# Output tiles between the last pairs' value products, two reads moved: a gated cross-attention block on one Trainium2 core

## The chip, the core and the metric

The kernel runs on one core of one Trainium2 chip. The time is device microseconds of one launch. Before the change three runs took 1480.28, 1481.79 and 1483.81 us; their median, 1481.79 us, is the time before. The profile is of one further execution, of 1480.91 us.

## The reference

32 sequences of 64 tokens attend to a context of the same size, with 32 heads of 128 channels, and a linear layer with low-rank adapters follows. Cut to what is computed:

```
x  = x + tanh(g_xattn) * attn(layernorm(x), ctx, mask, bias)
       q, k, v = layernorm(x) @ Wq, ctx @ Wk, ctx @ Wv         # 512 -> 32 heads x 128
       score   = q k^T / sqrt(128) + bias, masked
       attn    = (softmax(score) @ v) @ Wo                      # 4096 -> 512
x  = x + tanh(g_ffn) * (layernorm(x) @ weight^T + bias + adapter(layernorm(x)))
```

All of it is in fp32.

## The kernel before

The 2048 tokens are done in two phases (`p` = 0, 1) of 1024 tokens, each 8 tiles of 128 tokens. A phase first makes keys and values of all heads (`stage_a`), which go to DRAM, and then runs `attention`, whose inner function `run` goes over 16 pairs of heads, `n` = 0 to 15. After phase 1 the linear layer (`ffn_chunk`) runs over four chunks of 512 tokens.

Every large product is split in a high and a low part: `mm3` (L94 to L101) makes of each term three matmuls, high x high, high x low and low x high. A tile of output of one pair has two terms and so six matmuls of 128x128 by 128x512 into one bank of PSUM; the order inside a tile is (ah,bh), (ah,bl), (al,bh) for the first term, then the same for the second, and `last` puts chosen ones at the end. For pair `n` the parts of the attention are:

- `q_unit(n)`: queries of the pair, 42 matmuls.
- `score(n, ...)` with `scores` (L855): small products of queries and keys, then on VectorE the addition of the bias and a maximum (L863, L865), on GpSimd the subtraction of the maximum (L866), on ScalarE the exponential (L875, through `exped`, one step later).
- `normed` (L879): per head a sum, a reciprocal and a product on VectorE (L885 to L887), then the multiplication of the 128x512 block on GpSimd (L888). `turn` (L899) transposes in blocks of 32 on VectorE and 8 small copies (L896) bring the blocks to their places in `pt` (or `pz`). For the last two pairs all of this is one generator, `last_turned`: at its step 0 and 2 it does `normed` for the two heads of pair 14, at 4 and 5 it transposes these, at 6 and 8 it does `normed` for pair 15.
- `pv(n)`: small products of the turned probabilities with the values (L1010) into four banks; of each bank ScalarE makes the high part (L1014, `ch` or `cx`) and VectorE the low part (L1015, `cl` or `cx`), and after each comes a `beat()`. It then asks for the values of pair `n+1` (L804).
- `prep_o(n)`: the output weights `wo` of a pair are split, high on ScalarE, low on GpSimd (L91, for pair 13 L1034 and L1038), and when both halves are done the next pair's raw weights are fetched (L259), into the same buffer.
- `oproj(n)` and `oproj2(n, ...)`: output tiles `pa`. `oproj2` accumulates two pairs `n` and `n+1` in one bank, and VectorE adds the bank to `acc` (L1074).

The program's order is written out by hand and each engine executes its own instructions in that order. Work that accompanies the matmuls is written as generators in the list `streams`; `beat()` advances every one of them by a step, after each unit or tile. `drain(g)` runs a generator to its end at that place. So the place of a `beat()` decides where, in the queues of VectorE, ScalarE, GpSimd and SP, a step's instructions stand. All DMAs go through SP's queue; one that waits holds up those behind it.

[...] A new tile takes the bank that was given back first, by the program's order; this is how the banks of the built program follow one another, for instance 6, 7, 1, 2 for the scores of pairs 14 and 15 and 4, 3, 5, 0 for the products of pair 13.

At the end of a phase `run` does: the scores of 14 and 15, a beat, the drain of `ob[13]` (which splits `wo` of pair 13), `pv(13)`, then `last_unit` (which adds generators of the next phase, in phase 1 `ffn_weights`), then the tiles of pairs 12 and 13, `pv(14)`, `pv(15)`, and the tiles of pairs 14 and 15. Generators are set aside in `held` while `pv(14)` and `pv(15)` run.

In the linear layer the normalized tokens of phase 1 are turned by `ffn_turn(t)` and stored in DRAM (`xtd`, L1279), and `ffn_load(c, ...)` reads a chunk of them back in four steps of four DMAs each (L1262), one step per beat. `ffn_split` makes the high part on ScalarE and the low part on VectorE (`fa`, L90 and L91), `ffn_lora` does the eight matmuls of the adapters (`pt`, L1286 and L1287), `ffn_out` does a tile (`pf`, 12 matmuls and 2 of L1314, the sum on VectorE at L1316, the store at L1317) and then a beat.

Of the kernel before, what the change touches and what calls it, by code (L numbers as in the profile page):

```python
# [14 lines left out]
ALU = mybir.AluOpType  # L15
AX = mybir.AxisListType

P = 128
# [25 lines left out]
def flamingo_block(ctx: ExitStack, tc: tile.TileContext, x, xT, ctxT, bias, mask, gx, gf,  # L44
# [19 lines left out]
    def beat():  # L64
        for g in list(streams):
            if next(g, True):
                streams.remove(g)

    def drain(g):
        if g is not None and g in streams:  # L70
            streams.remove(g)
            for _ in g:
                pass
# [12 lines left out]
    def psum(name, shape=(P, 512)):  # L86
        return psp.tile(list(shape), F32, tag="ps", name=name)
# [6 lines left out]
    def mm3(ps, terms, start=True, stop=True, last=()):  # L94
        todo = []
        for (ah, al), (bh, bl) in terms:
            todo += [(ah, bh), (ah, bl), (al, bh)]
        todo = [x for k, x in enumerate(todo) if k not in last] + [todo[k] for k in last]
        for i, (a, b) in enumerate(todo):
            nc.tensor.matmul(ps, a, b, start=start and i == 0, stop=stop and i == len(todo) - 1,  # L100
                             skip_group_check=True)  # L101
# [693 lines left out]
    def attention(p, res, rest, qt, freed):  # L795
# [251 lines left out]
        def o_terms(n, t):  # L1047
            h, lo = ctx_of(n)
            w = b["o", n]
            sl = slice(t * P, (t + 1) * P)  # L1050
            return [((h[:, i, sl], lo[:, i, sl]),
                     (w[:, 0, i * 512:(i + 1) * 512], w[:, 1, i * 512:(i + 1) * 512])) for i in range(2)]

        def oproj(n, ts=range(NT)):
            drain(ob.get(n))
            for t in ts:
                ps = psum(f"pa{p}_{n}_{t}")
                mm3(ps, o_terms(n, t))
                nc.vector.tensor_tensor(acc[t], ps, acc[t], ALU.add)  # L1059
                beat()  # L1060


        def oproj2(n, ts, lead, beside=None):
            drain(ob[n])
            ts = list(ts)
            for group in [ts[:lead]] + [[t] for t in ts[lead:]]:
                ps = [psum(f"pa{p}_{n}_{t}") for t in group]
                for k, t in enumerate(group):
                    mm3(ps[k], o_terms(n, t), stop=False)
                    beat()  # L1070
                drain(ob[n + 1])
                for k, t in enumerate(group):
                    mm3(ps[k], o_terms(n + 1, t), start=False)
                    nc.vector.tensor_tensor(acc[t], ps[k], acc[t], ALU.add)  # L1074
                    if n == NPR - 2 and p < NPH - 1:
                        nc.sync.dma_start(out=x1d[t * P:(t + 1) * P, :], in_=acc[t])
                    beat()
                    if beside:
                        beside(t)

        ob, qT = {}, {}

        def start_o(n, wait=0):
            ob[n] = behind(wait, prep_o(n)) if wait else prep_o(n)
            streams.append(ob[n])


        def run(xq, prefetch, before_last, last_unit, values_read, beside=None):
            qb = {}


            def start_q(n, eng=nc.gpsimd, wait=0):
                g = p * NPR + n
                qb[n] = prep("q", g, eng, wait, then=(lambda: fetch("q", g + 1, "r0")) if n + 1 < NPR else None)
                streams.append(qb[n])

            def q_unit(n):
                g = p * NPR + n
                drain(qb.get(n))
                if n == 0:  # L1100
                    start_q(1, nc.vector, 2)
                elif n == NPR - 1:
                    before_last()
                elif n % 2 == 0 or n == 3:
                    start_q(n + 1)
                qT[n] = kqp.tile([P, 2, TP], F32, tag="kq", name=f"qT{g}")
                if n == 1:
                    start_o(0, 2)
                end = unit(wt[("q", g)], xq, None, k_dst(qT[n]), f"q{g}", tuple(carry))
                carry.clear()  # L1110
                end()
                if n % 2 and 3 < n < NPR - 1:
                    start_q(n + 1)

            def score(*ns):
                for n in ns:
                    drain(b.get(("m", n)))
                for n in ns:
                    for i in (0, 1) if n else (1, 0):
                        scores(n, i, qT[n], b["k", n])  # L1120
                for n in ns:
                    if 0 < n < NPR - 2:
                        load_k(n + 2)
                n = ns[0]
                if n == 0:
                    b["s", n] = first_softmax()
                elif n == NPR - 2:
                    b["s", n] = b["s", n + 1] = last_turned()
                else:
                    b["s", n] = both(normed(n, 1), turned(n))  # L1130
                streams.append(b["s", n])
                if 1 < n < NPR - 2:
                    b["n", n + 1] = normed(n + 1, 5)
                    streams.append(b["n", n + 1])

            q_unit(0)
            enter_late()
            b["m", 1] = bias_mask(1)
            score(0)
            streams.append(b["m", 1])  # L1140
            streams.append(load_acc())
            q_unit(1)
            start_q(2)
            pv(0)
            score(1)
            oproj(0)
            q_unit(2)
            start_o(1)
            pv(1)
            q_unit(3)  # L1150
            score(2, 3)
            for a in range(4, NPR, 2):
                oproj(a - 3)
                q_unit(a)
                start_o(a - 2)
                pv(a - 2)
                q_unit(a + 1)
                if a < NPR - 2:
                    oproj(a - 2)
                start_o(a - 1)  # L1160
                if a < NPR - 2:
                    pv(a - 1)
                else:
                    drain(b["s", a - 1])
                    next(ob[a - 1])
                    held = list(streams)
                    streams.clear()
                score(a, a + 1)
                if a == NPR - 8:
                    streams.append(paced(prefetch(), 4))  # L1170

            n = NPR - 4
            load_v(n + 3)
            beat()
            streams.append(ob[n + 1])
            drain(ob[n + 1])
            pv(n + 1)
            streams.extend(g for g in held if g is not ob[n + 1])
            last_unit()
            start_o(n + 2, 3)  # L1180
            oproj2(n, range(4), 4)
            start_o(n + 3, 3)
            oproj2(n, range(4, NT), 1)
            drain(ob[n + 3])
            drain(b["s", n + 3])
            held = list(streams)
            streams.clear()
            pv(n + 2)
            pv(n + 3)
            streams.extend(held)  # L1190
            values_read(acc)
            oproj2(n + 2, range(NT), 2, beside)

        return enter, run

# [39 lines left out]
    def ffn_weights(tags):  # L1235
        wf = [big(tags[i], [P, KT, 512], F32R, f"wf{i}") for i in range(2)]
        ffn_w.update(wf=wf, tags=tags)
        streams.append(ffn_load(0, tags[6]))
        ar, br, a2 = ffn_w["ar"], ffn_w["br"], ffn_w["a2"]

        b2 = ffn_w["b2"] = [wbp.tile([P, 512], F32R, tag="wb", name=f"b2{i}") for i in range(2)]
        for _ in range(8):
            yield
        nc.scalar.copy(b2[0], br)
        nc.scalar.copy(b2[1][64:P, :], br[64:P, :])
        nc.gpsimd.tensor_tensor(b2[1][0:64, :], br[0:64, :], b2[0][0:64, :].bitcast(F32), ALU.subtract)
        yield
        nc.scalar.copy(a2[:, :, 0:NL * R], ar)
        nc.gpsimd.tensor_tensor(a2[:, :, 64:64 + NL * R], ar, a2[:, :, 0:NL * R].bitcast(F32), ALU.subtract)
        yield  # L1250
        for kt in range(KT):
            split(ffn_w["raw"][:, kt, :], wf[0][:, kt, :], wf[1][:, kt, :], nc.gpsimd)
            yield
        streams.append(paced(x1_load(1), 2))
# [75 lines left out]
    for p in range(NPH):  # L1330
# [34 lines left out]
        else:  # L1365
# [29 lines left out]
            def load(c, tag):  # L1395
# [6 lines left out]
                          3: [(ffn_turn, 4)]})  # L1402
            ffn_chunk(1, {0: [(ffn_turn, 5)],
                          1: [(ffn_turn, 6)],
                          2: [(ffn_turn, 7), (ffn_split, 2, 0, 1)],
                          3: [(load, 3, "f0"), (ffn_split, 2, 2, 3)]})
            ffn_chunk(2, {2: [(ffn_split, 3, 0, 1)],
                          3: [(ffn_split, 3, 2, 3)]})
            ffn_chunk(3)
# [45 lines left out]
```

## Time and profile before

| what | value |
|---|---|
| median of three runs | 1481.79 us |
| profiled execution, its own time | 1480.91 us |
| its span | 1479.1 us |
| TensorE (PE) busy | 1467.4 us, 99% |
| GpSimd (POOL) busy | 1051.8 us, 71% |
| VectorE (DVE) busy | 938.2 us, 63% |
| ScalarE (ACT) busy | 713.8 us, 48% |
| granted clock of TensorE | 1.0 |
| one 128x128 by 128x512 matmul of a `pa` tile, start to start | 0.227 us |
| `pv` of one pair, unstalled | 2.02 to 2.04 us |

The page of a profile gives busy times, what moved by DMA, the chain of work that ended last, and groups of instructions with the idle time before them. The timeline lists the instructions of one engine in order of time, merged where one follows another: start, duration, engine, line, operation, what is written from what, the count, and in brackets the idle time before it and what ended that. "issue" there means that the engine waited for nothing that the profile shows. The view of the waits lists who waited for whom: total, number of times, longest.

### The profile page before, as it was taken

To read this page: it belongs to the slowest core of one execution; us is meant where nothing else is said; L and a number is where in the kernel's file an instruction comes from. 1 tells how busy PE (TensorE), PEld (TensorE's weight loads), DVE (VectorE), ACT (ScalarE), POOL (GpSimd) and SP (SyncE) were. 2 spreads that over 40 slices of the span, in tenths; PEclk is the share of its full clock that TensorE was granted. 3 is DMA by queue.
4 is the path that set the end of the run, shared out by engine and by line. 5 is a ranking of instruction groups with operands and counts; after the bars stand their busy time and mean duration, and the time that the engine had idled before them with its cause. 6 is when DMAs were issued, how large, how long until landed. Compare 5 with 4: busy or idle time off the path is not lost.

```text
span 1479.1 us, 31285 instructions
## 1 busy us (share of the span) xinstructions
PE 1467.4 (99%) x12008; PEld 1221.3 (83%) x12008; DVE 938.2 (63%) x1589; ACT 713.8 (48%) x1582; POOL 1051.8 (71%) x1160
## 2 busy tenths in 40 slices
PE   9999999999999999999999999999999999999998
PEld 7888888888888888888888888888888888888887
DVE  5675464367776677676379756436767667767774
ACT  5444233346645664576334423334655566557611
POOL 4899378968766676778889947896876767677420
PEclk9999999999999999999999999999999999999999
DMA  5754544475443455352385664447544345535454
GB/s 204 285 203 163 183 174 165 142 276 175 159 156 122 151 193 194 112 190 93 141 288 208 235 218 178 172 142 256 188 155 166 117 155 183 204 117 178 116 145 111
DMA packets 148343, 259.38 MB, mean 175 GB/s; under 512 B 44417, under 2 KB 78209, under 8 KB 144098
## 3 DMA queue, kind: packets, MB, share of 16 engines
q1 hardware_dynamic: 147906, 256.87, 50.3%
q8 instruction: 94, 1.54, 0.4%
q10 hardware_dynamic: 288, 0.52, 0.1%
q14 instruction: 55, 0.45, 0.1%
HBM read 179.74 MB, written 77.61 MB: 174 GB/s over the span
## 4 chain that ended last, share of the span: by engine, by line
PE 94%; DMA 2%; SPq 1%; POOL 1%; ACT 1%; issue 1%; DVE 1%; POOLq 0%; ACTq 0%; DVEq 0%
PE pa L100 22%; PE pvv L100 6%; PE pxv L100 6%; PE pzv L100 6%; PE pxq L100 6%; PE pvq L100 6%; PE pzk L100 6%; PE pvk L100 6%; PE pxk L100 6%; PE pzq L100 6%; PE po L1010 4%; PE ps L861 4%; PE pyv L100 3%; PE pyq L100 3%; PE pyk L100 3%; PE pf L100 2%
## 5 line engine op out<-in xcount | busy, mean ns | idle before, releaser
L100 PE MATMUL pa<-wo,ch 128*128 128x512 f32 x896 | 278.4, 392 | 0.7 <-ACT ch L1014 0.4
L896 ACT COPY pt<-tp 32x256 f32<-32x256 f32 x452 | 182.4, 404 | 69.7 <-DVE tp L899 60.1
L100 PEld LDWEIGHTS pa<-wo,ch 128*128 128x128 f32 x896 | 166.8, 188 | 36.2 <-ACT ch L1014 0.7
L100 PE MATMUL pa<-wo,cl 128*128 128x512 f32 x448 | 174.9, 390 | 0.2 <-DVE cl L1015 0.2
L1059 DVE TENSOR_TENSOR acc<-pa,acc 128x512 f32<-128x512 f32 x192 | 129.4, 681 | 53.4 <-PE pa L100 53.4
L815 POOL TENSOR_TENSOR sm<-sm,madd 128x512 f32<-128x512 f32 x60 | 77.2, 1296 | 92.8 <-DMA sm<-bias 92.8
L888 POOL TENSOR_TENSOR sm<-sm,r 128x512 f32<-128x512 f32 x64 | 67.0, 1047 | 71.5 <-DVE r L887 67.5
L351 DVE TENSOR_TENSOR vt<-pvv,vt 128x512 f32<-128x512 f32 x64 | 44.2, 691 | 103.4 <-PE pvv L100 103.4
L1015 DVE TENSOR_TENSOR cl<-po,ch 128x512 fp32r<-128x512 f32 x112 | 74.6, 689 | 46.8 <-ACT ch L1014 46.4
L100 PEld LDWEIGHTS pa<-wo,cl 128*128 128x128 f32 x448 | 84.1, 188 | 19.2 <-DVE cl L1015 1.8
L866 POOL TENSOR_TENSOR sm<-sm,mx 128x512 f32<-128x512 f32 x64 | 67.2, 1051 | 38.1 <-DVE mx L865 37.9
L351 DVE TENSOR_TENSOR qT<-pvq,qT 128x512 f32<-128x512 f32 x64 | 44.1, 690 | 62.5 <-PE pvq L100 60.9
L373 ACT COPY vt<-pxv 128x512 f32<-128x512 f32 x32 | 18.8, 589 | 130.9 <-PE pxv L100 130.9
L351 DVE TENSOR_TENSOR kT<-pvk,kT 128x512 f32<-128x512 f32 x60 | 41.1, 686 | 57.2 <-PE pvk L100 56.9
L875 ACT ACTIVATE sm<-sm 128x512 f32<-128x512 f32 x62 | 39.2, 633 | 78.2 <-POOL sm L866 78.2
L91 POOL TENSOR_TENSOR wo<-rawo,wo 128x512 fp32r<-128x512 f32 x56 | 71.5, 1299 | 1.6 <-ACT wo L90 1.5
L1010 PEld LDWEIGHTS po<-pt,v 64*64 64x64 f32 x3840 | 59.7, 135 | 13.1 <-issue 11.9
L1014 ACT CAST ch<-po 128x512 fp32r<-128x512 f32 x112 | 63.0, 594 | 12.4 <-PE po L1010 12.4
L1010 PE MATMUL po<-pt,v 64*64 64x64 f32 x3840 | 64.2, 220 | 3.2 <-issue 3.0
L861 PE MATMUL ps<-kB,qT 128*64 128x64 f32 x2048 | 65.3, 223 | 1.2 <-issue 1.0
L861 PEld LDWEIGHTS ps<-kB,qT 128*64 128x64 f32 x2048 | 62.1, 138 | 4.9 <-issue 3.2
L351 DVE TENSOR_TENSOR vt<-pzv,vt 128x512 f32<-128x512 f32 x64 | 44.2, 691 | 34.1 <-PE pzv L100 33.6
(999 smaller groups left out, 3864.3 us busy)
## 6 DMA issues: line engine op xcount, KB each, us to landing
kd<-kT SPq DMA_DIRECT2D x64, 512.0 KB, 3.9
vd<-vt SPq DMA_DIRECT2D x128, 256.0 KB, 2.4
kB<-kd SPq DMA_DIRECT2D x32, 1024.0 KB, 9.9
v<-vd SPq DMA_DIRECT2D x32, 1024.0 KB, 8.0
rawq<-wq SPq DMA_DIRECT2D x32, 512.0 KB, 3.7
sm<-bias SPq DMA_DIRECT2D x64, 256.0 KB, 4.9
rawo<-wo SPq DMA_DIRECT2D x32, 512.0 KB, 3.8
rawk<-wk SPq DMA_DIRECT2D x31, 512.0 KB, 5.5
```

What stands on the lines that cost most here:

```text
L91: eng.tensor_tensor(lo, raw, hi.bitcast(F32), ALU.subtract)
L100: nc.tensor.matmul(ps, a, b, start=start and i == 0, stop=stop and i == len(todo) - 1, skip_group_check=True)
L351: nc.vector.tensor_tensor(o, ps, i, ALU.add)
L815: nc.gpsimd.tensor_tensor(t, t, masks[p][0], ALU.add)
L861: nc.tensor.matmul(ps[h * S:(h + 1) * S, t, :], qT[:, i, tok], kT[:, i, tok], start=True, stop=True)
L866: nc.gpsimd.tensor_tensor(s, s, mx.unsqueeze(2).to_broadcast([P, NT, S]), ALU.subtract)
L888: nc.gpsimd.tensor_tensor(t, t, r.unsqueeze(2).to_broadcast([P, NT, S]), ALU.mult)
L896: f(pts[n == NPR - 2][dst, i, :, qi * 32:(qi + 1) * 32], of[src, :, ki * 32:(ki + 1) * 32])
L1010: nc.tensor.matmul(ps[h][d:d + S, k, :], v[keys, t, i * P + d:i * P + d + S], pt[keys, i, t, :], start=True, stop=True)
L1014: nc.scalar.copy(o, ps[h])
L1015: nc.vector.tensor_tensor(l, ps[h], o.bitcast(F32), ALU.subtract)
L1059: nc.vector.tensor_tensor(acc[t], ps, acc[t], ALU.add)
```

## The change

`oproj2` no longer takes a range of tiles and a lead; it takes an order, a list of entries `(k, t)`, where `k` is 0 for the tile's first pair and 1 for its second, and of functions that are called at their place. Four things follow from it or come beside it:

1. The first halves of tiles 0 and 1 of pair 12 stand between the scores of pairs 14 and 15 and `pv(13)`.
2. The second half of tile 7 (pair 13) stands between `pv(14)` and `pv(15)`; `hold`, which sets the generators aside, stands ahead of `pv(14)` as before, and so one half tile sooner.
3. `ffn_weights` adds `ffn_load(0)` to the streams at its seventh step and no longer at its first. In `ffn_chunk(1)`, `load` of chunk 3 is called at tile 2 and no longer at tile 3.
4. In `oproj(0)` the tile 0 has its two matmuls with the low part of the products (`al`) last.

```diff
-                mm3(ps, o_terms(n, t))
+                mm3(ps, o_terms(n, t), last=(2, 5) if n == 0 and t == 0 else ())
...
-        def oproj2(n, ts, lead, beside=None):
+        def oproj2(n, order, beside=None):
             drain(ob[n])
-            ts = list(ts)
-            for group in [ts[:lead]] + [[t] for t in ts[lead:]]:
-                ps = [psum(f"pa{p}_{n}_{t}") for t in group]
-                for k, t in enumerate(group):
-                    mm3(ps[k], o_terms(n, t), stop=False)
+            ps = {}
+            for x in order:
+                if callable(x):
+                    x()
+                    continue
+                k, t = x
+                if k == 0:
+                    ps[t] = psum(f"pa{p}_{n}_{t}")
+                    mm3(ps[t], o_terms(n, t), stop=False)
                     beat()
+                    continue
                 drain(ob[n + 1])
...
-            pv(n + 1)
-            streams.extend(g for g in held if g is not ob[n + 1])
-            last_unit()
-            start_o(n + 2, 3)
-            oproj2(n, range(4), 4)
-            start_o(n + 3, 3)
-            oproj2(n, range(4, NT), 1)
-            drain(ob[n + 3])
-            drain(b["s", n + 3])
-            held = list(streams)
-            streams.clear()
-            pv(n + 2)
-            pv(n + 3)
+
+            def between():
+                pv(n + 1)
+                streams.extend(g for g in held if g is not ob[n + 1])
+                last_unit()
+                start_o(n + 2, 3)
+
+            def hold():
+                drain(ob[n + 3])
+                drain(b["s", n + 3])
+                held[:] = streams
+                streams.clear()
+
+            oproj2(n, [(0, 0), (0, 1), between, (0, 2), (0, 3), (1, 0), (1, 1), (1, 2), (1, 3),
+                       lambda: start_o(n + 3, 3)]
+                   + [(k, t) for t in range(4, NT - 1) for k in range(2)]
+                   + [(0, NT - 1), hold, lambda: pv(n + 2), (1, NT - 1), lambda: pv(n + 3)])
             streams.extend(held)
             values_read(acc)
-            oproj2(n + 2, range(NT), 2, beside)
+            oproj2(n + 2, [(0, 0), (0, 1), (1, 0), (1, 1)] + [(k, t) for t in range(2, NT) for k in range(2)], beside)
...
-        streams.append(ffn_load(0, tags[6]))
...
-        for _ in range(8):
+        for k in range(8):
+            if k == 6:
+                streams.append(ffn_load(0, tags[6]))
             yield
...
-                          2: [(ffn_turn, 7), (ffn_split, 2, 0, 1)],
-                          3: [(load, 3, "f0"), (ffn_split, 2, 2, 3)]})
+                          2: [(ffn_turn, 7), (load, 3, "f0"), (ffn_split, 2, 0, 1)],
+                          3: [(ffn_split, 2, 2, 3)]})
```

In this call `n` is 12, and `NT` is 8. The count of instructions on every engine is unchanged.

## Prediction

> **What bounds the kernel now.** I read the busy times first: TensorE is busy 1467.4 of 1479.1 us at full clock, so all that an order of work can give is in the 11.7 us between. Of these 1.3 lie ahead of the first matmul and 3.2 behind the last. The view of TensorE's waits names most of the rest, and the list of DMA queues one fact that goes with it:
>
> ```profile
> PE po L1010 <- issue: 3.0, 4, 1.2
> PE pt L1286 <- ACT fa L90: 1.6, 1, 1.6
> PE pa L100 <- DVE cl L1015: 0.2, 1, 0.2
> PE po L1010 <- DMA v<-vd: 0.2, 1, 0.2
> q8 instruction: 94, 1.54, 0.4%
> ```
>
> All four places of `po` are in the last pairs' products with values. The chain at the end of phase 0 shows two of them:
>
> ```profile
> 651.51 8.19 DMA v<-vd
> 659.70 0.04 issue
> 659.75 2.09 PE po L1010 x127
> 661.83 1.20 issue
> ...
> 663.30 21.98 PE pa L100 x96
> 685.28 2.48 PE po L1010 x156
> 687.76 0.88 issue
> 688.64 1.73 PE po L1010 x100
> 690.37 21.98 PE pa L100 x96
> ```
>
> Unstalled, a `pv` takes 2.03 us. Here `pv(13)` takes 3.60 from 659.70, and 14 and 15 together 5.09 for 4.06. In phase 1 the same places have 0.28 and 0.61 us of "issue".
>
> What is this wait? Queue q8 moved 94 packets in 1.54 MB, 16,384 bytes each. TensorE has 12,008 matmuls and 12,008 weight loads, 94 times 255.5. Counting both through the trace, every "issue" stretch of TensorE (those of the scores too) begins at instruction 193 or 194 modulo 256. So q8 brings TensorE's instructions in blocks of 256, and the wait is for a block. The DMA packets agree: those ahead of the four waits end at 661.67, 687.26, 1363.82 and 1389.46, and TensorE resumes 1.36, 1.38, 1.56 and 1.25 us later. A packet begins when TensorE is about 312 instructions ahead of that block's start, plus usually 1.0 to 1.4 us (2.05 and 3.36 at two of the four). From that point to the resumption it was 4.68, 3.41, 3.66 and 5.53 us. The values' products use 126 instructions a microsecond (the scores 66), 312 of them in 2.5 us, and starve; a tile of six matmuls uses 12 in 1.36 us and gives time.
>
> [...]
>
> **The change part by part.** First the end of each phase. Its least time before is 3.88 (scores) + 3 x 2.03 + 16 half tiles x 1.36 + 0.23, together 31.96 us. The 0.23 is the first matmul behind small products: 21.98 for 96 `pa` matmuls against 21.76 at 0.2267. Phase 0 took 34.87 (655.50 to 690.37), 2.91 over it: 0.32 for the values `v` of pair 13, 1.57 and 1.03 for blocks. Phase 1 took, to the end of `pv(15)`, 33.87 (1359.24 to 1393.11, which is the start of pair 15's first matmul, 1396.06, less 2.72 and 0.23): 1.91 over it, 0.66 and 0.76 for blocks and 0.45 behind, most of it low parts `cl` come late.
>
> (1) *Two half tiles ahead of `pv(13)`, one ahead of `pv(15)`.* They need only `ch`, `cl` of pair 12 and `wo`, done long before. Time from the point of request to the block's start becomes, in phase 0, 5.7 us for `pv(13)` (58 instructions of scores, 2.95 for tiles, 230 of products) and 4.0 for `pv(15)`; in phase 1 5.8 and 4.6. Against 4.68, 3.41, 3.66 that is enough; against 5.53, the last, it isn't by 0.9, but then the request stood behind the reads of `xt` and `wo`, see (3). I take 0.15 as left of it. The values of pair 13 land during the tiles. Price: two more changes from small to large products in a phase, 2 x 0.23 = 0.46. Without a new wait phase 0 gains 2.91 - 0.46 = 2.45 and phase 1 1.91 - 0.46 = 1.45.
>
> But **a new wait** comes. Two beats now stand ahead of `pv(13)`, so `last_turned` is two steps further inside it: step 5, the transpose of pair 14's second head, now precedes the fourth low part `cx` on VectorE (before, both transposes came behind it). Phase 1 before:
>
> ```profile
> 1368.09 2.55 POOL L1038 TENSOR_TENSOR wo<-rawo,wo 128x512 fp32r<-128x512 f32 x2
> 1370.81 1.05 POOL L888 TENSOR_TENSOR sm<-sm,r 128x512 f32<-128x512 f32 x1 [0.17 <-DVE r L887]
> 1370.59 1.27 DVE L1015 TENSOR_TENSOR cx<-po,cx 128x512 fp32r<-128x512 f32 x2
> 1371.78 1.29 DVE L899 STREAM_TRANSPOSE tp<-sm 128x512 f32<-128x512 f32 x2
> ```
>
> That transpose needs the multiplication L888, which still stands behind the two L1038: 1370.64 + 1.05 = 1371.7; the transpose 0.65 and the low part 0.68 end at 1373.05. The sixth matmul of the first tile of pair 13 reads it. TensorE would be there at 1359.24 + 3.88 + 2.95 + 2.03 + 2.95 + 1.13 = 1372.2. It loses 0.9 and 0.1 of restart, 1.0. Phase 0 by the same steps: low part at 669.3, TensorE at 668.5, 0.95 lost. Behind the transpose wait only that low part and sums with slack. Bounds: none if the multiplication is sooner by 0.9; 1.5 if VectorE runs late.
>
> Net: phase 0 +1.5, phase 1 +1.45 - 1.0 - 0.15 = +0.3. Banks: given back in order, `pv(15)` takes banks of tiles 4 to 6 and of `pv(14)`, not tile 7's, so no wait. The softmax's steps end at the same count of half tiles; `pz` and `pt` were done at 1380.4 and 1383.8, over 3 us ahead of `pv(14)`. In phase 0 the next phase's steps run three beats fewer before it; what is late, VectorE's two subtractions L475 and the low parts on GpSimd after them, shifts some 4 us, and GpSimd's last low part comes at about 717 for a matmul at 720.
>
> (2) *Two low-part matmuls last in `oproj(0)`, tile 0.* There the third matmul came 0.16 late behind `cl` and the next had a restart: 1042.877, 1043.266, 1043.599 against steps of 0.227, so 0.27 each phase, **0.54** in all. The 0.21 ahead of the first, for `ch`, stays.
>
> (3) *`ffn_load(0)` behind the fetch of pair 15's `wo`.* SP's queue, before:
>
> ```profile
> 1371.71 13.44 SPq L1262 DMA_DIRECT2D xt<-xtd  x16
> 1385.25 0.43 SPq L259 DMA_DIRECT2D rawo<-wo  x1
> ```
>
> The fetch also needs GpSimd to be done with pair 14's weights, 1380.1, so it goes 5 us sooner and lands near 1384. ScalarE, which waited for it until 1389.11 with `ch` of `pv(14)` behind, is free near 1388. This is what removes the 0.45 counted above. The 16 reads follow from 1380.5 at 0.53 each to 1389 and land by 1391.4; ScalarE first wants them at about 1394.
>
> (4) *Chunk 3's reads a tile sooner.* The chain before:
>
> ```profile
> 1456.78 0.36 SPq L1317
> ...
> 1458.78 2.19 DMA xt<-xtd
> 1461.12 0.63 ACT fa L90
> 1461.77 0.70 DVE fa L91
> 1462.52 0.50 PE pt L1287
> ```
>
> Each step of reads stands behind a tile's store, which waits for that tile. One tile is 3.17 us: the last read lands at 1457.8, its high part is ready at 1458.6 and its low part, behind VectorE's sum of tile 2, at 1459.2, where TensorE wants them at 1460.0 and 1460.24. The eight `pt` and the restart took 4.20 (1458.65 to 1462.85) for 1.81, so **2.38** go. The first step is now behind the store of `xq` of tile 7, 1442.25 + 2.0, and SP reaches it at 1444.3: nothing.
>
> **Sum.** 1.5 + 0.3 + 0.54 + 2.38 = 4.7 us. The span goes from 1479.1 to 1474.4, the profiled execution from 1480.9 to 1476.2; the median shown is 0.9 above the profiled one, so **1477.1**. Two kernels less than 0.2% apart (3.0 us) can't be told from each other here: one kernel's runs spread over 3.5 us.
>
> **Rivals.** *No new wait on VectorE* (GpSimd quicker, or the tiles later): 1.95 more, 1475.2. For it: the estimate rests on two GpSimd times, which are rough. Against: three instructions in a row that each wait for the one before.
>
> [...] The 1.57, 1.03, 0.66 and 0.76 stay and the changes of product size are paid: phase 0 0.32 - 0.46 = -0.15, with no wait for `cx` since TensorE is late anyway; phase 1 0.45 - 0.46 - 0.3 = -0.3. With (2) and (4) 2.5 us, 1479.3: no change. Against it is the place modulo 256.
>
> *The end's wait moves elsewhere*: with SP held by another store or the low part behind VectorE's sum, (4) gives nothing: 2.3 us, 1479.5, no change.
>
> *Slower: `xt` of chunk 0 comes too late.* Its reads begin 9 us later. ScalarE and VectorE work in order, and the first `pt` needs all four at about 1412. At 0.53 each there are 20 us to spare; the first ones before, with values in flight, took 0.65, 1.11, 2.58 and 1.97. From 1.9 a read (16 x 1.9 = 30 us, 1413 with the landing) it costs, and at 2.4 it costs 8, which ends at 1485. Against: the values of pair 14 are in before 1380.
>
> **How the numbers follow.** Chances: forecast 0.57, no new wait 0.13, rule holds 0.12, end's wait stays 0.11, slower 0.07. Faster by over 0.2% (below 1478.8) are the first two but for 0.03 of scatter: 0.67; within 0.2% 0.26; slower 0.07. The range goes from 1474.4, the second less 0.8 of scatter between medians, to 1480.4, the third and fourth with it; it leaves out the slower and some tails.
>
> **What would show it.** Right: no "issue" of TensorE in `po` of pairs 13 to 15 in either phase; in its place about 0.8 before the sixth matmul of the first `pa` with `cx`, released by VectorE's L1015, twice; `pt` of chunk 3 without a wait; L259 at about 1380 ahead of the 16 L1262. Wrong: "issue" in the same blocks, a wait of `po` for a bank, or a wait for `fa` or `xt` in the last chunk, or behind `pv(15)`.

## The result and the profile after

The changed kernel takes 1477.5 us, the median of 7 runs (1476.51 to 1478.16); the kernel before took 1482.18 us beside it, again in 7 runs (1480.28 to 1483.81). The ratio is 0.9967, with a 95% interval of 0.9955 to 0.9979: 0.33% faster. The profiled execution has a span of 1475.7 us for 1479.1.

TensorE's waits after the change (what waited, for whom, total us, times, longest):

```profile
PE ps L861 <- issue: 2.0, 4, 0.8
PE pa L100 <- DVE cx L1015: 1.1, 2, 0.8
PE ppk L100 <- DVE c0b L91: 0.5, 1, 0.5
PE pa L100 <- ACT ch L1014: 0.4, 2, 0.2
```

The "issue" of `po`, the wait of `pt` for ScalarE's `fa`, that of `pa` for `cl` and that of `po` for the values are gone. In their place stands what the prediction had put there, a wait of `pa` for the low part `cx`, twice. The other rows were there before or vary from execution to execution: "issue" before scores (1.2 us before with its short stretches, 1.8 now, without the one at 660.35), the high part `ch` (0.4 in both), and a low part in the first products of all.

The chain at the end of phase 0, from the multiplication of pair 14's second head on:

```profile
667.64 1.01 POOL sm L888
668.65 0.02 issue
668.67 0.71 DVE tp L899
669.38 0.59 DVE cx L1015
669.97 0.04 issue
670.01 14.14 PE pa L100 x61
684.15 2.04 PE po L1010 x128
686.19 1.59 PE pa L100 x6
687.78 2.03 PE po L1010 x128
689.81 21.98 PE pa L100 x96
```

The lower half shows the benefit: `pv(14)` and `pv(15)` each take 2.03 to 2.04 us, with a half tile of 1.59 between (1.36 and the 0.23 for the change of size). The upper half shows the price: multiplication (`sm`, L888), transpose (`tp`, L899) and low part (`cx`, L1015), each waiting for the one before, and TensorE at their end.

VectorE at the same place of phase 1:

```profile
1369.03 0.65 DVE L1015 TENSOR_TENSOR cx<-po,cx 128x512 fp32r<-128x512 f32 x1
1370.79 0.71 DVE L899 STREAM_TRANSPOSE tp<-sm 128x512 f32<-128x512 f32 x1 [1.10 <-POOL sm L888]
1371.42 0.65 DVE L1015 TENSOR_TENSOR cx<-po,cx 128x512 fp32r<-128x512 f32 x1
```

The transpose waits 1.10 us for GpSimd, and the fourth low part, whose data is ready (ScalarE's last high part ended at 1368.64), stands behind it. SP's queue has the fetch first now, and the last chunk's `pt` runs through:

```profile
1379.36 0.35 SPq L259 DMA_DIRECT2D rawo<-wo  x1
1379.76 9.59 SPq L1272 DMA_DIRECT2D xt<-xtd  x16
```

### The profile page after: what moved, and what is told of

Read it like the earlier page. It is cut to its first block, busy times and chain, and to the rows that moved or that the text cites. A ratio compares the mean times of both kernels' runs of the same rounds, so it can differ in the third digit from the quotient of the medians.

```text
span 1475.7 us, 31292 instructions
## 1 busy us (share of the span) xinstructions
PE 1467.0 (99%) x12008; PEld 1220.4 (83%) x12008; DVE 940.2 (64%) x1589; ACT 714.6 (48%) x1582; POOL 1052.0 (71%) x1160
## 4 chain that ended last, share of the span: by engine, by line
PE 97%; DVE 1%; issue 1%; ACT 1%; POOL 0%; DMA 0%; SPq 0%; DVEq 0%; POOLq 0%
PE pa L100 23%; PE pxq L100 6%; PE pvq L100 6%; PE pvv L100 6%; PE pxv L100 6%; PE pzv L100 6%; PE pzq L100 6%; PE pzk L100 6%; PE pvk L100 6%; PE pxk L100 6%; PE po L1010 4%; PE ps L861 4%; PE pf L100 3%; PE pyq L100 3%; PE pyv L100 3%; PE pyk L100 3%
## 5 line engine op out<-in xcount | busy, mean ns | idle before, releaser
L888 POOL TENSOR_TENSOR sm<-sm,r 128x512 f32<-128x512 f32 x64 | 66.8, 1044 | 72.5 <-DVE r L887 70.2
L1015 DVE TENSOR_TENSOR cl<-po,ch 128x512 fp32r<-128x512 f32 x112 | 74.5, 689 | 47.6 <-ACT ch L1014 47.2
L91 POOL TENSOR_TENSOR wo<-rawo,wo 128x512 fp32r<-128x512 f32 x56 | 71.4, 1299 | 3.1 <-ACT wo L90 3.1
L1010 PEld LDWEIGHTS po<-pt,v 64*64 64x64 f32 x3840 | 59.2, 135 | 10.8 <-issue 9.3
L187 POOL TENSOR_TENSOR vs<-wvr,wvr 128x512 f32<-128x512 f32 x24 | 32.1, 1348 | 49.3 <-DMA wvr<-wv 49.3
```

What stands on the lines that cost most here:

```text
L91: eng.tensor_tensor(lo, raw, hi.bitcast(F32), ALU.subtract)
L888: nc.gpsimd.tensor_tensor(t, t, r.unsqueeze(2).to_broadcast([P, NT, S]), ALU.mult)
L1010: nc.tensor.matmul(ps[h][d:d + S, k, :], v[keys, t, i * P + d:i * P + d + S], pt[keys, i, t, :], start=True, stop=True)
L1015: nc.vector.tensor_tensor(l, ps[h], o.bitcast(F32), ALU.subtract)
```

## The experiments

Three stretches of TensorE's timeline serve as a finer measure than whole runs, which scatter by about 3.5 us. P0 and P1 run from the first score of pair 14 to the first matmul of the next stage, the keys of phase 1 or the adapters of the linear layer. "Last `pt`" runs from the first adapter matmul of chunk 3 to its first `pf`. By the durations of the prediction, P0 and P1 take at least 53.95 us in the old order (3.88 for scores, 6.09 for three `pv`, 32 half tiles of 1.36, two changes from small to large products at 0.23) and 54.41 in the new one (four changes).

| kernel | P0 | P1 | last `pt` | median, us | ratio to before, 95% |
|---|---|---|---|---|---|
| before | 56.75 | 55.93 | 4.20 | | |
| changed | 55.45 | 55.84 | 1.81 | 1477.5 | 0.9967 (0.9955 to 0.9979) |
| tiles_only | 55.44 | 55.45 | 4.65 | 1483.5 | 1.0001 (0.9993 to 1.0009) |
| reads_only | 56.46 | 54.93 | 1.81 | 1479.0 | 0.9974 (0.9957 to 0.9990) |
| xt_ahead | 55.49 | 56.06 | 1.81 | 1478.2 | 0.9961 (0.9946 to 0.9976) |
| turn_behind | 54.38 | 54.41 | 1.81 | 1476.2 | 0.9950 (0.9933 to 0.9966) |
| blocks_early | 54.32 | 54.37 | 1.81 | 1474.4 | 0.9955 (0.9942 to 0.9967) |
| changed_again | 55.53 | 55.63 | 1.81 | 1478.4 | 0.9969 (0.9959 to 0.9980) |
| shift_before | 56.35 | 55.96 | 4.21 | | |
| shift_after | 55.44 | 55.59 | 1.81 | | |

The kernel before had a median of 1483.1 us beside tiles_only to turn_behind, and 1482.0 beside blocks_early and changed_again.

A stretch is of one execution, and it scatters too. reads_only changes nothing ahead of the linear layer, and shift_before only what comes ahead of everything; yet with the old order P0 took 56.75 us in the kernel before, 56.46 in reads_only and 56.35 in shift_before, and P1 55.93, 54.93 and 55.96. The new order, with the transpose where the change left it, took 55.44 to 55.53 in P0, which is a gain of 0.8 to 1.3 us, and 55.45 to 56.06 in P1, which shows no gain.

**tiles_only.** The kernel before with the new order of tiles alone: steps (2), (3) and (4) of the prediction are taken back. The cut of the edit is against the changed kernel.

```diff
-                mm3(ps, o_terms(n, t), last=(2, 5) if n == 0 and t == 0 else ())
+                mm3(ps, o_terms(n, t))
...
+        streams.append(ffn_load(0, tags[6]))
...
-        for k in range(8):
-            if k == 6:
-                streams.append(ffn_load(0, tags[6]))
+        for _ in range(8):
             yield
...
-                          2: [(ffn_turn, 7), (load, 3, "f0"), (ffn_split, 2, 0, 1)],
-                          3: [(ffn_split, 2, 2, 3)]})
+                          2: [(ffn_turn, 7), (ffn_split, 2, 0, 1)],
+                          3: [(load, 3, "f0"), (ffn_split, 2, 2, 3)]})
```

> The kernel before with the new order of output tiles alone (part 1); the reads and the order inside tile 0 stay as before. Block theory: no "issue" of TensorE inside pv(13) and pv(14), the new wait of 0.5 to 1.1 us before the sixth matmul of pair 13's first tile in both phases, and in phase 1 the late low parts and a late block at pv(15), as the reads of xt still stand ahead of the fetch of wo. Gain 0.3 to 1.3 us, within 0.2%; 1.6 us of the last chunk's wait stays. If instruction blocks have nothing to do with it [...], "issue" of about 1.2, 0.9, 0.3 and 0.6 us stays inside the products and the kernel is 0.5 us slower.

TensorE's waits in it:

```profile
PE pt L1295 <- ACT fa L90: 2.1, 1, 2.1
PE pa L100 <- DVE cx L1015: 1.5, 2, 0.8
PE ps L861 <- issue: 1.0, 3, 0.5
```

No "issue" in `po`, the wait for `cx` twice, 0.69 and 0.79. The late low parts and the late block that I expected at `pv(15)` didn't come: it took 2.03 us. P0 is 1.3 us shorter than before, P1 0.5 and the last `pt` 0.45 longer, which makes 1.3 in all. The whole kernel shows no difference: its interval allows a gain of 1.0 us at most, and the traced execution, 1479.34 us, was the fastest of 22. So a gain of the tiles alone is shown in P0, not in the kernel's time. The tiles move the wait away and spend more than half of it: of the 2.80 us over the least time in P0 1.03 remain over the new one and 0.46 went for the changes of size.

**reads_only.** The kernel before with the read of chunk 3 one tile sooner, step (4).

```diff
-                          2: [(ffn_turn, 7), (ffn_split, 2, 0, 1)],
-                          3: [(load, 3, "f0"), (ffn_split, 2, 2, 3)]})
+                          2: [(ffn_turn, 7), (load, 3, "f0"), (ffn_split, 2, 0, 1)],
+                          3: [(ffn_split, 2, 2, 3)]})
```

> The kernel before with chunk 3's read called at tile 2 alone. My step: the wait for fa in the last chunk goes, 2.4 us faster, and the "issue" in the products stays at about 3.0 us in all. Rival (the wait moves elsewhere): under 1 us, with a wait of pt or pf in the last two chunks.

The last `pt` takes 1.81 for 4.20, 2.39 less, and the median falls by 4.1 us, and its interval (1.5 to 6.4) contains the 2.4. "issue" in `po` was 2.2 us, two times, and none in phase 1 in this execution, so that this part varies. One chunk earlier the eight `pt` of chunk 2 took 2.49 for 1.82, with a wait of 0.23 for VectorE's low part `fa`. The changed kernel's own traces have 1.82 and 2.07 there, but shift_before, with the read at its old place, has 2.50, so that the moved read need not be the cause.

Where the other 1.7 us of the 4.1 may come from is seen in the clock. In shift_before, whose last `pt` waits as in the kernel before (1.62 and 0.22 us), TensorE ran at half its clock for 3.4 us soon after. Each line gives a stretch and its length, TensorE's busy time and matmuls in it, its granted clock, and the DMA's share and GB/s:

```profile
1477.00:1481.00 4.00, 2.16 (x9) 1.00 0.13 21
1481.00:1484.40 3.40, 3.40 (x10) 0.50 0.20 77
1484.40:1488.00 3.60, 3.60 (x17) 1.00 0.21 77
```

Most matmuls in the middle stretch come 0.43 us apart for 0.23, so that about 1.7 us are lost. The other executions of these kernels have no trace, but each has its mean granted clock. With the wait in the last `pt` (the kernel before in its two groups of runs, and tiles_only) it was under 1.0 in 43 of 64; without it (the changed kernel, reads_only, xt_ahead, turn_behind, blocks_early, changed_again) in 1 of 38. The median of the kernel before, beside reads_only, was 1481.5 us at 1.0 and 1483.2 at 0.999. So in many executions the wait goes with a lower clock, and with more lost than its 2.39 us. That the clock fell at this place in all of them isn't shown; the kernel before and tiles_only were traced at 1.0.

**xt_ahead.** The changed kernel with the reads of `xt` ahead of the fetch of `wo` again.

```diff
+        streams.append(ffn_load(0, tags[6]))
...
-        for k in range(8):
-            if k == 6:
-                streams.append(ffn_load(0, tags[6]))
+        for _ in range(8):
             yield
```

> The changed kernel with ffn_load(0) back at the first step of ffn_weights. If putting it behind the fetch of wo was worth the 0.45 of late low parts and part of a late block, this is 0.5 to 1.5 us slower than the changed kernel (1478.0 to 1479.0), all of it between 1385 and 1396 us. If the move gave nothing, as the tile between pv(14) and pv(15) covers the late wo by itself, it is within 0.3 us of it.

P1 is 56.06, where the changed kernel has 55.84 and 55.63, and tiles_only, which also has the reads ahead, 55.45. The median of 1478.2 is at the lower end of what the first theory allowed, and changed_again, in another group of runs, has 1478.4. So no gain from this move is shown; the scatter of 1.0 us in P1 would hide one. One wait does change: with the reads ahead, `po` of `pv(15)` waits 0.27 us for VectorE's `cl`, and `pv(15)` takes 2.61 us, where the changed kernel has a late block and takes 2.39 and, in changed_again, 2.18.

**turn_behind.** The changed kernel with the second transpose one step later, behind the fourth low part.

```diff
-                if k in (4, 5):
-                    turn_next(n, k - 4)
+                if k in (4, 6):
+                    turn_next(n, (k - 4) // 2)
```

> The changed kernel with the transpose of pair 14's second head at step 6 of last_turned and no longer at step 5, so that it stands behind the fourth low part of pv(13) on VectorE. If the new wait is the transpose's (my step), both waits of pa for cx go, 0.57 and 1.09 us in the changed kernel's trace: 1.7 us faster, 1475.8. Rival: the low part is late by ScalarE's high part or by banks, and the wait stays within 0.3 us. Second rival: the later transpose delays the probabilities of pair 14 or 15, and TensorE waits for pt or pz at pv(14) or pv(15) instead.

VectorE in phase 1, four low parts with only the first transpose among them:

```profile
1369.60 1.29 DVE L1015 TENSOR_TENSOR cx<-po,cx 128x512 fp32r<-128x512 f32 x2
1370.81 0.70 DVE L899 STREAM_TRANSPOSE tp<-sm 128x512 f32<-128x512 f32 x1
1371.43 1.25 DVE L1015 TENSOR_TENSOR cx<-po,cx 128x512 fp32r<-128x512 f32 x2
```

Both waits for `cx` are gone, and `pv(14)` and `pv(15)` wait for no `pz` or `pt` (one of 0.3 us for `pt` stands at 1065, at the start of phase 1's pairs). Both rivals are refuted. P0 and P1 are 54.38 and 54.41, the least time of this order: nothing is lost there in this execution. That is 1.07 and 1.43 us less than in the changed kernel; the waits for `cx` account for 0.57 and 1.09 of it, and the rest are blocks of instructions that came in time here. The median is 1476.2, but the trace has a new wait, at the start of phase 1:

```profile
PE ps L861 <- issue: 3.2, 4, 1.1
PE pxk L100 <- DVE c1p L91: 0.8, 2, 0.6
```

With its restarts it costs 1.4 us: the first five products of phase 1 (six matmuls each) start in step with the kernel before, and from the seventh on they are 1.40 us behind it. xt_ahead and shift_after have the same wait.

**shift_before and shift_after.** The kernel before, and the changed one, with 32 small matmuls ahead whose result isn't used. They cost time themselves (13.7 us in shift_before); one execution each, read for the place of the waits alone.

```diff
+    for i in range(32):
+        nc.tensor.matmul(warm[:, :8], ident, ident[:, :8], start=True, stop=True)
```

> The kernel before with 32 small matmuls (128x128 by 128x8, result unused) behind the first warming ones: 128 instructions of TensorE (64 matmul passes and 64 weight loads) more, ahead of everything. Block theory: every "issue" stretch of TensorE moves with the block, from instruction 194 to 66 modulo 256: in phase 0 from the last product of pv(13) to its middle, with 0 to 0.9 us, and from pv(15)'s first quarter to its third quarter; none stays at its old place in the program. If the wait belongs to the place (the values' load, contention, the products themselves), it stays at the end of pv(13) and 28 products into pv(15).

The chain of shift_before at the end of phase 0 (two lines were added, so that L1010 is L1012 here):

```profile
671.96 3.88 PE ps L863 x128
675.84 1.08 PE po L1012 x63
676.92 0.92 issue
677.84 1.20 PE po L1012 x65
679.04 21.99 PE pa L100 x96
701.03 3.41 PE po L1012 x220
704.44 1.17 issue
705.61 0.80 PE po L1012 x36
```

In the kernel before the waits came after 127 and after 156 products; here they come after 63 and after 220. 128 instructions are 64 products (TensorE has 12,072 matmuls and as many weight loads here, for 12,008): the waits have stayed at their place in the stream of instructions, still 193 or 194 modulo 256 when the added ones are counted, and so have moved through the program. In phase 1 they are 0.06 and 1.68 us. The wait belongs to the block of instructions and not to the place in the program.

One thing about this count has to be added to step 1. It comes out only when TensorE's semaphore and drain instructions, 184 in the kernel before, are counted with the matmuls and weight loads (24,200 in all, 94.5 blocks). With matmuls and weight loads alone the waits of the kernel before stand at places that drift from 124 down to 18 modulo 256.

> The changed kernel with the same 32 small matmuls ahead. Block theory: the time from request to block start is 6.6 us at pv(13) and 4.0 at pv(15) in phase 0, against 3.4 to 3.7 that a block took, so the interposed tiles also cover this alignment: no "issue" over 0.4 us inside the products of pairs 13 to 15. If the tiles only helped at one alignment, stretches of 0.5 us or more come back.

```profile
PE ps L863 <- issue: 2.2, 5, 0.7
PE pa L100 <- DVE cx L1017: 1.6, 2, 0.8
PE pxk L100 <- DVE c1p L91: 0.8, 2, 0.6
```

No "issue" in `po` at this alignment either. So the tiles cover the blocks at the two alignments tried; the wait for `cx` is there in both phases.

**blocks_early.** turn_behind with the next phase's generators as far as they were in the kernel before.

```diff
-                keys = prep("k", g, nc.gpsimd, 18, then=lambda: fetch("k", g + 2, "r0"))
+                keys = prep("k", g, nc.gpsimd, 15, then=lambda: fetch("k", g + 2, "r0"))
+                for _ in range(3):
+                    next(blocks)
                 streams.extend((blocks, keys))
```

> turn_behind with the next phase's generators three beats further at their start: blocks is advanced three steps in last_unit, and the keys' weights wait 15 beats for 18. In the traces of turn_behind and xt_ahead, two low parts of VectorE at the start of phase 1 (c1p, L91) took 6.7 us for 1.3 while GpSimd worked, and TensorE lost 1.4 us to them (0.8 as a wait of pxk at about 717). If the cause is that GpSimd's subtractions and low parts, some 4 us late by the three missing beats, fall on them, these two take 1.3 us here as in the kernel before, TensorE has no wait at the first pxk, and the median is 0.5 to 1.4 us under turn_behind's: 1475.2. Rival: the stretch has another cause (a bank, the late casts of ScalarE) and comes back here. In all against the kernel before: 6 to 8 us faster.

First VectorE and GpSimd at the start of phase 1 in turn_behind, then VectorE in blocks_early:

```profile
712.19 6.73 DVE L91 TENSOR_TENSOR c1p<-c,c1p 128x512 fp32r<-128x512 f32 x2
...
710.80 2.56 POOL L475 TENSOR_TENSOR c<-c,c 128x512 f32<-128x512 f32 x2
713.29 2.56 POOL L91 TENSOR_TENSOR c1p<-c,c1p 128x512 fp32r<-128x512 f32 x2
715.78 0.76 POOL L294 TENSOR_TENSOR wk17p<-rawk,wk17p 128x256 fp32r<-128x256 f32 x1
716.48 0.76 POOL L283 TENSOR_TENSOR wsk<-rawk 128x256 f32<-128x256 f32 x1
```

```profile
709.84 1.28 DVE L91 TENSOR_TENSOR c1p<-c,c1p 128x512 fp32r<-128x512 f32 x2
```

Two low parts of VectorE that take 1.28 us alone took 6.73 while GpSimd worked without a pause; the first of them alone took 5.59. In blocks_early GpSimd was idle from 706.9 to 710.8, and they took 1.28 again; they meet GpSimd for their last 0.3 us only. The rival, another cause that would come back, is refuted. TensorE's waits in blocks_early are all that is left in the kernel:

```profile
PE warm L514 <- POOL ident masks.py:199: 1.3, 1, 1.3
PE ps L861 <- issue: 0.6, 2, 0.4
PE pa L100 <- ACT ch L1014: 0.4, 2, 0.2
```

The median is 1474.4 us, 0.45% under the kernel before, and its profiled span 1470.9. turn_behind, in the other group of runs, is 0.50% under it, so that the whole times don't show the 1.4 us between the two; the traces do.

**changed_again.** The changed kernel once more, beside blocks_early.

> The changed kernel once more, beside blocks_early on the same chip: 4 to 5 us faster than the kernel before and 1.5 to 3 us slower than blocks_early, by the waits of pa for cx (1.7 us) and, in some executions, the stretched low parts (1.4 us). If its trace has the stretch, the share of executions that pay it is not small.

1478.4 for 1474.4, 4.0 us apart, more than the 1.5 to 3 that I expected. Its waits for `cx` were 0.82 and 0.83. The two low parts took 5.33 us in it, without a wait of TensorE for them; in the first trace of the changed kernel they took 3.39. What makes up the rest of the 4.0 isn't shown: beside the waits for `cx`, its trace has 1.2 us more of "issue" before scores than that of blocks_early, and the first four matmuls of 128x512 took 2.95 us for 1.88. Both vary from execution to execution.

## Why the prediction was right

1477.1 was forecast, 1477.5 measured, and the signs named in advance came: no long "issue" in the products, a wait for `cx` twice, no wait in the last `pt`. That the two figures lie 0.4 us apart is in part luck. Between the profiled executions, both at a granted clock of 1.0, only 3.4 us of the 4.7 were gained. The medians differ by 4.7 because that of the kernel before lies 1.3 us above its profiled execution (1482.18 for 1480.91) and that of the changed kernel doesn't (1477.5 for both), where I had added 0.9 to both. A clock that falls behind the last chunk's wait, as in shift_before (3.4 us at 0.50), would explain it, as the kernel before was traced at 1.0. By terms the sum is so:

| step | predicted | measured |
|---|---|---|
| P0, tiles and new wait | 1.5 | 56.75 - 55.45 = 1.30 |
| P1, tiles, new wait and `wo` | 0.3 | 55.93 - 55.84 = 0.09 |
| tile 0 of `oproj(0)`, both phases | 0.54 | 0.26 + 0.25 = 0.51 |
| last chunk's reads | 2.38 | 2.39 |
| sum | 4.7 | 4.3 |

The row of P1 lies inside the scatter of that stretch, 1.0 us. The remaining 0.9 us between 4.3 and 3.4 lies outside the change: "issue" before scores is 0.6 more in this execution, a low part in the first products costs 0.6, and two smaller waits are 0.3 less.

*The blocks* (step 1) were read rightly: "issue" of `po` went from 3.0 us to a single 0.05, and shift_before shows the cause. The term "0.15 left of it" measured 0.36: `pv(15)` of phase 1 took 2.39 us for 2.03. Its packet began late, at 1387.92, while the reads of `xt` were being issued; that these held it up isn't shown.

*The rival in which the waits stay* (chance 0.12 in the prediction) is refuted: the "issue" in the products fell from 3.0 to 0.05 us, and the wait for `cx`, which it left out, came. In the kernel before, with 512 small instructions in a row, TensorE did starve for up to 1.2 us at a place. By the prediction's estimate from the packets' starts it had about 312 instructions in hand when it asked for the next block.

*The new wait* was forecast at 0.95 and 1.0 us and is, gap and restart together, 0.57 in phase 0 and 1.09 in phase 1. In phase 0 TensorE came later than reckoned, as a block fell on the last scores (0.23 of "issue" at 660.35); in changed_again none fell there, and the wait for `cx` was 1.09 with its restart. In the kernel before the same matmul was 0.13 late and the wait for the values hid it, so the 0.32 that I put down to the values was in part a block. turn_behind shows the chain of causes by removing it.

*The order of `wo` and `xt`* (step 3) is the step that wasn't borne out. The fetch did come 5.9 us sooner (5.0 when counted from the first score), as worked out, but the 0.45 us that I credited to it don't show. tiles_only, with the reads ahead, loses nothing there, so that the half tile between `pv(14)` and `pv(15)` can cover the late low parts alone; xt_ahead loses 0.57 in `pv(15)`, the changed kernel 0.36. Whether the move is worth anything stays open.

*What is late after three missing beats* (step 1, last sentences) was followed for GpSimd alone. Its last low part came at 716.98, where I had put it at about 717, in time. What I missed is that VectorE's two low parts at the same time would be stretched by it, to 3.4 us in this trace and to 6.7 in others, where they cost 1.4.

## What to carry to other kernels

Runs of 512 small instructions of TensorE waited here for the next block of 256: look for "issue" idle time that recurs at a fixed count of instructions, and put one large piece of ready work between two such runs; here that removed up to 1.6 us of waiting at a place, for 0.23 each time that TensorE changed from small to large products. When beats or tiles are moved across a step written out by hand, follow each engine's queue to the first instruction that waits and ask who stands behind it; here one transpose, a step too early, took back 0.6 to 1.1 us in each phase, and moving it one step later gave that back. Look at the granted clock behind a wait: in shift_before one of 1.8 us near the end was followed by 3.4 us at half clock, which cost about 1.7 us more. Work shifted on GpSimd was not free here even with slack of its own: two instructions of VectorE beside it took 3.4 to 6.7 us for 1.28, and TensorE lost 1.4 us where they took longest.

## What the runs showed of the hardware that I had not expected

In turn_behind two VectorE instructions (`c1p`, L91, both inputs in SBUF), which take 0.68 and 0.69 us in the kernel before, took 5.59 and 1.22 us when GpSimd's instructions followed one another without a pause: the first began at 712.19, and TensorE's matmul that waited for it began at 717.84; between the two GpSimd began five instructions, from 713.29 to 717.32. In the changed kernel's trace the ends of the two engines' instructions alternate, GpSimd's at 713.58, VectorE's at 714.13, GpSimd's at 715.28, VectorE's at 715.83, GpSimd's at 716.98. VectorE's two took 1.70 and 1.77 us there, and GpSimd's own were stretched too, from 1.30 to 1.74. A sum with one input in PSUM (`acc`, L1078), at 711.83 in the same trace, kept its 0.69 beside GpSimd. That the place of the inputs makes the difference isn't shown: no run changed it alone. In blocks_early the two meet for 0.3 us only: VectorE's keep their length (1.28 for both), and GpSimd's takes 1.48 for 1.28.
